# Second feed-forward in passes of 6, 13 and 13 token tiles, with two sequences split between passes

## The chip, the cores and the metric

The kernel runs on one core of a Trainium2 chip. The metric is the device time of one execution in microseconds (us). Three runs of the kernel before gave 700.61, 701.8 and 703.71 us; their median, 701.8 us, is the time before.

## The reference

Eight sequences of 512 tokens with 128 features go through a feed-forward with experts, an attention, and the same feed-forward again, each added to its input:

```python
x = x + 0.5 * ffn(layernorm(x))        # router, 8 experts of 128 -> 512 -> 128, each token to its best two
x = x + attention(layernorm(x))        # 16 heads of 8, causal
x = x + 0.5 * ffn(layernorm(x))        # the same weights

# ffn(x):
logits = x @ router_w + router_b
topk_scores, topk_idx = top_k(logits, 2)
gates = softmax(topk_scores)
# for each expert e of a token's two:  y += gate_e * (relu(x @ W1[e] + b1[e]) @ W2[e] + b2[e])
```

All arrays are float32.

## The kernel before, in words

The kernel computes each expert only for the tokens that chose it. A sequence is four tiles of 128 tokens (`T` = 4). A *pass* (class `Group`, L449) takes some sequences, gives each expert a room of `cap` rows in a buffer in DRAM (`xs`), scatters every normalised token to two of these rooms, and runs the eight experts over their rooms. There are six passes (L1362 to L1367): f0, f1, f2 for the first feed-forward, g0, g1, g2 for the second. The f and the g passes each take two, three and three whole sequences, with rooms of 351, 480 and 480 rows. A room is computed in `ct` tiles of equal size: 351 is three tiles of 117 rows, 480 is four of 120.

`route` (L801) does one sequence of a pass: layernorm, transposes, router logits, rank of each expert, and a running count that gives each token its row in its two rooms (`to`, L866); `seen` carries the counts from one sequence of the pass to the next. It then enters eight scatters (`scatter`, L874), one for each tile and rank, as jobs for GpSimd (POOL). `close_group` (L916) checks that no room overflowed. If one did, a flag set in `verdict` (L1272) sends the program to the general path (L1549), which computes everything densely.

`experts` (L924) is a generator of *pieces*. For an expert e, `turn` (L972) transposes the room's tiles on TensorE (lines L976 and L980, tiles xbT_ps and xT), four pieces `wide` (L986, tile z, L989) multiply by a quarter of W1 and evict with ReLU on ScalarE (L996) or VectorE (L998), and `ct` pieces `out` (L1010, tile y, L1013) multiply by W2 and add the bias on VectorE (L1017, tile ysb). The pieces of expert e + 1's first part and expert e's `out` pieces alternate. `pieces` (L461) is their number: 65 for g0, 73 for each pass of 480 rows. The rows come from DRAM by `fetch` (L931, tile xb), issued on SP.

The results go back in two ways. An untagged pass (f0, f1, f2, g0) stores each expert's room in order (L1024, SP), and `combine` (L1064) gathers two rows for each token with indirect DMAs on GpSimd (`gather`, L1084) and adds them to x with the gates (`add`, L1071). A tagged pass (g1, g2) carries with each row its destination; `homes` (L939) computes it, `send` (L956) scatters the results token by token with indirect DMAs on GpSimd, and `collect` (L1099) loads them for a whole sequence from SP (tile yr, L1110), adds on VectorE (L1114) and stores the output (L1120).

The order is written out by hand in `macaron_kernel`. Attention is 96 units (8 sequences x 4 groups of heads x 3 steps, L1394); before it lie 30 units without attention, after it 30 more (`first`, `core`, `tail`, `ends`, L1399). `plan` (L1421) says which pass lends its pieces to which units:

```python
        plan = [
            (f0, first, first, -16), (f1, -17, -16, 7), (f2, 5, 7, 43), (g0, 41, 43, 79),
            (g1, 78, 79, tail - 1), (g2, tail - 2, tail - 1, ends),
        ]
```

The second number is the unit in which rooms are fetched first, the third and fourth bound the units that take pieces. `surround` (L1427) builds a unit: the scores on TensorE (`scores`, L1192, lines L1201 and L1208), the values of the unit before (L1227), one piece, the causal mask, then what is due in this unit (parts of `route`, `project`, `operands`, `finish`, put there by `at`), and further pieces up to the quota, which is the pieces left over the units left, rounded up. So g0's 65 pieces fill 36 units. One scatter, gather or send is issued in each unit by `transfer` (L650), more if they are urgent. Each waits for the latest eviction in the program's order (`mark`, `behind_mark`, L635). VectorE, ScalarE, TensorE and SP follow the order of the program.

Other names that the steps touch: rooms are listed in `ROOMS` (L49) with the number of sequences, the rows and whether tagged; g0 reuses f1's. `clear` (L687) and `clear_results` (L705) zero the rooms of g1 and g2 and their results early in the attention (`later`, L557).

Of the kernel before, what the change touches and what calls it, by code (L numbers as in the profile page):

```python
# [13 lines left out]
I32 = mybir.dt.int32  # L14
# [34 lines left out]
ROOMS = [(2, 351, False), (3, 480, False), (3, 480, False), (3, 480, True), (3, 480, True)]  # L49
# [399 lines left out]
class Group:  # L449


    def __init__(self, seqs, cap, key, xs, ys, tagged):
        self.seqs, self.cap, self.key, self.xs, self.ys = seqs, cap, key, xs, ys
        self.tagged, self.width = tagged, D + 2 * tagged
        self.ct = -(-cap // P)
        self.rows = cap // self.ct
        assert self.ct * self.rows == cap
        self.parts = [(t, min(3 if cap > 4 * P else 4, self.ct - t))
                      for t in range(0, self.ct, 3 if cap > 4 * P else 4)]
        self.placed = 0  # L460
        self.pieces = E * (len(self.parts) * (1 + C) + self.ct) + 1  # L461
# [21 lines left out]
class Main:  # L483
    def __init__(self, tc, ctx, aps):
# [37 lines left out]
        for i, (n, cap, tagged) in enumerate(ROOMS):  # L522
            self.xs.append(self.tc.dram_tile([E * n * N, D + 2 * tagged], FP, name=f"xs_{i}"))

            self.ys.append(self.tc.dram_tile(
                [2 * n * N * tagged + E * cap, D], FP, name=f"ys_{i}"
            ))
# [80 lines left out]
        self.ops, self.o_tok, self.normal, self.whole = {}, {}, {}, {}  # L608
# [96 lines left out]
    def clear_results(self, i):  # L705
        dst = self.ys[i][: 2 * ROOMS[i][0] * N, :].rearrange("(p a r) d -> p a (r d)", p=P, r=4)
        self.nc.sync.dma_start(
            dst, self.zeros[:, : 4 * D].unsqueeze(1).to_broadcast([P, dst.shape[1], 4 * D])
        )
# [80 lines left out]
    def open_group(self, seqs, cap, i, key):  # L790
        const = self.const
        g = Group(seqs, cap, key, self.xs[i], self.ys[i], ROOMS[i][2])
        assert len(seqs) <= ROOMS[i][0] and cap <= ROOMS[i][1]
        assert not g.tagged or cap == ROOMS[i][1]
        g.to = const.tile([P, len(g.seqs), T, 2], I32, name=f"to_{key}")
        g.back = const.tile([P, len(g.seqs), T, 2], I32, name=f"back_{key}")
        g.gates = const.tile([P, len(g.seqs), T, 2], FP, name=f"gates_{key}")
        g.seen = const.tile([P, E], BF, name=f"seen_{key}")
        return g

    def route(self, g, i, urgent=False, ahead=False, early=False):  # L801

        nc, small, tc = self.nc, self.small, self.tc
        b = g.seqs[i]
        key = f"{g.key}_{b}"
        if b in self.normal:
            xn = self.normal.pop(b)
        else:
            xn = yield from self.layernorm(self.x[b], key)
# [34 lines left out]
        nc.tensor.matmul(pos, self.earlier, mask, start=True, stop=False)  # L844
        for t in range(T - 1):
            nc.tensor.matmul(
                pos[:, t + 1 :, :], self.ones,
                mask[:, t : t + 1, :].to_broadcast([P, T - 1 - t, E]),
                start=False, stop=(i == 0 and t == T - 2),
            )  # L850
        if i > 0:
            nc.tensor.matmul(
                pos, self.ones, g.seen.unsqueeze(1).to_broadcast([P, T, E]),
                start=False, stop=True,
            )
# [10 lines left out]
        nc.vector.tensor_reduce(g.to[:, i], sm, AX.X, ALU.max)  # L866
        nc.vector.tensor_scalar(g.back[:, i], g.to[:, i], E * g.cap - 1, None, ALU.min)
        if g.tagged:
            nc.vector.tensor_copy(xn[:, :, D], g.to[:, i, :, 0])
            nc.vector.tensor_scalar(  # L870
                xn[:, :, D + 1], self.place, float(2 * N * i), None, ALU.add
            )

        def scatter(t, r):  # L874
            ins = nc.gpsimd.indirect_dma_start(  # L875
                out=g.xs[:, :],
                out_offset=bass.IndirectOffsetOnAxis(ap=g.to[:, i, t, r : r + 1], axis=0),
                in_=xn[:, t, : g.width], in_offset=None,
            ).ins
            tc.declare_no_dep(ins, group=f"xs_{g.key}", reason="no row has two tokens")  # L880
            tc.add_to_no_dep_group(f"xs_{g.key}", ins)
            self.in_turn(ins, scatter=True)
            self.behind_mark(ins)
            g.placed += 1

        self.enter([partial(scatter, t, r) for t in range(T) for r in range(2)], urgent, ahead)

        with nc.allow_low_precision(reason="counts of at most 32, exact in bf16"):
            by_e = mask.rearrange("p t e -> p e t")
            if i == 0:  # L890
                nc.vector.tensor_reduce(g.seen, by_e, AX.X, ALU.add)
            else:
                more = small.tile([P, E], BF, tag="more", name=f"more_{key}")
                nc.vector.tensor_reduce(more, by_e, AX.X, ALU.add)
                nc.vector.tensor_tensor(g.seen, g.seen, more, ALU.add)
# [16 lines left out]
        nc.vector.reciprocal(g.gates[:, i, :, 0], tot)  # L912
        nc.vector.tensor_tensor(g.gates[:, i, :, 1], g.gates[:, i, :, 0], e2, ALU.mult)
        yield

    def close_group(self, g, k):  # L916

        assert g.placed == 2 * T * len(g.seqs)
        nc = self.nc
        cp = self.bank([P, 512], f"cnt_ps_{g.key}")  # L920
        nc.tensor.matmul(cp[:1, :E], self.ones[:, 0:1], g.seen, start=True, stop=True)
        nc.vector.tensor_scalar(self.counts[:, k], cp[:1, :E], -float(g.cap), None, ALU.add)

    def experts(self, g):  # L924
# [14 lines left out]
        def homes(e, xb):  # L939
# [12 lines left out]
                home[e][:rows, : g.ct], row, float(2 * N * len(g.seqs) + e),  # L952
# [111 lines left out]
    def combine(self, g, i, dst=None, urgent=False, ahead=False):  # L1064

        nc = self.nc
        b = g.seqs[i]
        x = self.x[b]
        self.whole[b] = False

        def add(t, yts):  # L1071
            for r in range(2):
                nc.vector.scalar_tensor_tensor(
                    x[:, t, :], yts[r], g.gates[:, i, t, r : r + 1], x[:, t, :],
                    ALU.mult, ALU.add,
                )
            if t == T - 1:
                self.whole[b] = True
                if dst is not None:
                    nc.sync.dma_start(dst[b].rearrange("(t p) d -> p t d", p=P), x)  # L1080
# [3 lines left out]
        def gather(t, r):  # L1084
# [4 lines left out]
                    ap=g.back[:, i, t, r : r + 1], axis=0  # L1089
# [6 lines left out]
        self.enter([partial(gather, t, r) for t in range(T) for r in range(2)], urgent, ahead)  # L1096
        yield

    def collect(self, g, i, dst, parts=1):  # L1099

        nc = self.nc
        b = g.seqs[i]
        x = self.x[b]
        if i % 2 == 0:
            self.pair = self.p2.tile([P, 2, T, 2, D], FP, tag="ee", name=f"yr_{b}")
        yr = self.pair[:, i % 2]
        src = g.ys[2 * N * i : 2 * N * (i + 1), :].rearrange("(t p r) d -> p t r d", p=P, r=2)
        n = T // parts
        for k in range(parts):
            nc.sync.dma_start(yr[:, ts(k, n)], src[:, ts(k, n)])  # L1110
        yield
        for t in range(T):
            for r in range(2):
                nc.vector.scalar_tensor_tensor(  # L1114
                    x[:, t, :], yr[:, t, r], g.gates[:, i, t, r : r + 1], x[:, t, :],
                    ALU.mult, ALU.add,
                )
            if t % n == n - 1:
                k = t // n
                nc.sync.dma_start(  # L1120
                    dst[b].rearrange("(t p) d -> p t d", p=P)[:, ts(k, n)], x[:, ts(k, n)]
# [5 lines left out]
    def project(self, b):  # L1127
# [4 lines left out]
        assert self.whole[b], b  # L1132
# [171 lines left out]
def macaron_kernel(  # L1304
# [51 lines left out]
    with ExitStack() as main:  # L1356
# [5 lines left out]
        f0 = m.open_group([0, 1], 351, 0, "f0")  # L1362
        f1 = m.open_group([2, 3, 4], 480, 1, "f1")
        f2 = m.open_group([5, 6, 7], 480, 2, "f2")
        g0 = m.open_group([0, 1], 351, 1, "g0")
        g1 = m.open_group([2, 3, 4], 480, 3, "g1")
        g2 = m.open_group([5, 6, 7], 480, 4, "g2")  # L1367
        order = [f0, f1, f2, g0, g1, g2]
        place = {True: {}, False: {}}
        for g in order:  # L1370
            for i, b in enumerate(g.seqs):
                place[g.key[0] == "f"][b] = (g, i)
# [32 lines left out]
        def routed(u, g, i, urgent=False, ahead=False):  # L1405
            early = u < 0 or u > core
            r = m.route(g, i, urgent, ahead, early)
# [4 lines left out]
            if g is not f1:  # L1412
# [68 lines left out]
        with m.banks(("m", 8)):  # L1481

            n = [m.normalise(b) for b in range(5)]
            r = [m.route(f0, 0, early=True), m.route(f0, 1, early=True), m.route(f1, 0, True, early=True)]
# [11 lines left out]
            routed(first + 1, f1, 1, urgent=True)  # L1496
            routed(first + 3, f1, 2, urgent=True)
            routed(-22, f2, 0, urgent=True)
            combined(-16, f0, 0, urgent=True, ahead=True)
            routed(-14, f2, 1, urgent=True)  # L1500
            combined(-12, f0, 1, urgent=True)
            routed(-10, f2, 2, urgent=True)
            at(-10, m.project(0), 8)
            for b in range(B):
# [3 lines left out]
                elif b > 2:  # L1508
                    combined(u - (17 if b == 5 else 21), *place[True][b], urgent=b == 5, ahead=b == 5)
# [5 lines left out]
                routed(u + seq + (3 if b == B - 1 else 4), *place[False][b], urgent=b in (1, 4, 5, 6, 7), ahead=b in (4, 6, 7))  # L1515
            for i in range(2):
                combined(79 + 7 * i, g0, i, out)
            for i in range(3):
                at(tail + 2 + 3 * i, m.collect(g1, i, out), 5)
# [13 lines left out]
        with m.banks(("m", 8)):  # L1533
# [7 lines left out]
            last = [m.collect(g2, i, out, parts=2) for i in range(3)]  # L1541
# [55 lines left out]
```

## Time and profile before

| what | value |
|---|---|
| median of three runs | 701.8 us |
| profiled execution, its own time | 700.09 us |
| its span, first to last instruction | 698.3 us |
| mean granted TensorE clock | 0.977 |
| TensorE matmul busy | 629.2 us, 90% |
| f2 pass, first transpose to g0's first | 178.56 to 341.54 us |
| g0 pass, first transpose to g1's first | 341.54 to 493.97 us |
| g1 pass, its first transpose to its last matmul | 493.97 to 612.0 us |
| g2 pass, its first transpose to its last matmul | 616.69 to 677.5 us |
| last scatter of results lands | 683.35 us |

A page of the profile has the busy time of each engine, then the span in 40 slices (a digit is the busy share in tenths), the DMA queues, the chain of work that ended last, and the costliest groups of instructions. In the timeline each row is: start, duration, engine, line, operation, output<-inputs, shape, count, and in brackets the idle time before it with what ended it. Matmuls are pipelined, so durations of TensorE rows overlap; the start of the next row tells what one costs. A float32 matmul is recorded as two instructions, so a z piece has x2 and a y tile, four matmuls, has x8.

### The profile page before, as it was taken

How to read it: one execution, taken by the hardware profiler on the slowest of the kernel's cores; microseconds unless marked ns; L12 is line 12 of the kernel's file. 1: busy time of each engine (PE TensorE's matmuls, PEld its weight loads, DVE VectorE, ACT ScalarE, POOL GpSimd, SP SyncE). 2: the span in 40 equal slices, each digit the busy share in tenths (PEclk: the TensorE clock that was granted, in tenths of full speed). 3: DMA queues.
4: the chain of work that ended last, by engine and by line, in shares of the span. 5: the costliest groups of instructions: out<-in, count | busy, mean ns of one | idle time of the engine just before them, and what ended most of it. 6: DMA issues, size and time to landing. Idle time of an engine off the chain costs nothing. (4 is left out here: it accounts for less than half of the span.)

```text
span 698.3 us, 13045 instructions
## 1 busy us (share of the span) xinstructions
PE 629.2 (90%) x4867; PEld 410.3 (59%) x4867; DVE 410.2 (59%) x1442; ACT 341.3 (49%) x548; POOL 300.3 (43%) x322
## 2 busy tenths in 40 slices
PE   3269999999999999999999999999999998969980
PEld 2148867756465656556656656656456656747760
DVE  6736448734466666675687677676666654433414
ACT  4034443455755656565665565555665552234420
POOL 3744637642223223314154423424144556575660
PEclk9999999999999999999999999999999999889995
DMA  8747843312409921111211111101402111145324
GB/s 265 197 136 209 205 115 98 85 45 77 101 22 172 264 69 38 30 29 43 71 32 49 40 38 38 30 27 39 105 27 75 35 31 42 53 121 140 104 58 143
DMA packets 78670, 61.06 MB, mean 87 GB/s; under 512 B 7392, under 2 KB 70792, under 8 KB 78600
## 3 DMA queue, kind: packets, MB, share of 16 engines
q1 hardware_dynamic: 69608, 42.51, 23.8%
q0 software_dynamic: 8704, 17.63, 8.5%
q8 instruction: 41, 0.67, 0.4%
q14 instruction: 29, 0.24, 0.1%
q10 hardware_dynamic: 288, 0.01, 0.0%
HBM read 26.34 MB, written 33.78 MB: 86 GB/s over the span
## 5 line engine op out<-in xcount | busy, mean ns | idle before, releaser
L1208 ACT ACTIVATE ee<-st 128x768 f32<-128x768 f32 (+1 forms) x192 | 159.0, 881 | 104.1 <-PE st L1201 100.6
L474 POOL DMA_INDIRECT yt_f<-ys,back_f x64 | 64.8, 1013 | 133.5 <-DVE ee L1215 55.7
L1215 DVE TENSOR_TENSOR ee<-ee,keep 128x256 f32<-128x256 f32 (+1 forms) x192 | 93.5, 507 | 25.4 <-ACT ee L1208 25.3
L1013 PEld LDWEIGHTS y_g<-w_sb,h_g 128*120 128x120 f32 (+1 forms) x704 | 87.1, 184 | 27.4 <-issue 21.7
L875 POOL DMA_INDIRECT xs<-xn_g,to_g x64 | 63.8, 998 | 90.1 <-DVE ee L1215 34.9
L1013 PEld LDWEIGHTS y_f<-w_sb,h_f 128*120 128x120 f32 (+1 forms) x704 | 85.9, 182 | 28.5 <-issue 16.2
L1201 PE MATMUL st<-qT,kT 32*128 32x512 f32 (+3 forms) x1024 | 96.1, 467 | 2.3 <-ACT h_f L996 0.8
L1013 PE MATMUL y_f<-w_sb,h_f 128*120 128x128 f32 (+1 forms) x704 | 93.9, 277 | 0.2 <-DVE h_f L998 0.2
L989 PE MATMUL z_g<-xT_g,w_sb 128*128 128x480 f32 (+1 forms) x192 | 92.6, 569 | 1.3 <-ACT xT_g L980 1.3
L1013 PE MATMUL y_g<-w_sb,h_g 128*120 128x128 f32 (+1 forms) x704 | 93.0, 277 | 0.6 <-DVE o_tok L1250 0.3
L1227 PE MATMUL o<-ee,vpad 128*32 128x512 f32 (+3 forms) x1024 | 89.4, 442 | 0.8 <-DVE ee L1215 0.8
L989 PE MATMUL z_f<-xT_f,w_sb 128*128 128x480 f32 (+1 forms) x192 | 88.8, 551 | 1.0 <-ACT xT_f L980 1.0
L996 ACT ACTIVATE h_f<-z_f,b1T 128x480 f32<-128x480 f32 (+1 forms) x86 | 53.5, 623 | 68.2 <-PE z_f L989 67.3
L957 POOL DMA_INDIRECT ys<-ysb_g,home_g x64 | 63.7, 996 | 39.3 <-ACT h_g L996 8.7
L1017 DVE TENSOR_TENSOR ysb_f<-y_f,b_sb 120x128 f32<-120x128 f32 (+1 forms) x88 | 25.0, 287 | 77.9 <-PE y_f L1013 74.2
L996 ACT ACTIVATE h_g<-z_g,b1T 128x480 f32<-128x480 f32 (+1 forms) x71 | 45.7, 646 | 47.4 <-PE z_g L989 46.7
L1201 PEld LDWEIGHTS st<-qT,kT 32*128 32x128 f32 x1024 | 43.1, 183 | 32.6 <-issue 8.1
L1017 DVE TENSOR_TENSOR ysb_g<-y_g,b_sb 120x128 f32<-120x128 f32 (+1 forms) x88 | 25.1, 287 | 58.2 <-PE y_g L1013 57.6
L1227 PEld LDWEIGHTS o<-ee,vpad 128*32 128x32 f32 x1024 | 23.5, 108 | 52.4 <-issue 7.5
L875 POOL DMA_INDIRECT xs<-xn_n,to_f x40 | 39.0, 974 | 34.9 <-ACT xi_sb L727 8.1
L989 PEld LDWEIGHTS z_g<-xT_g,w_sb 128*128 128x128 f32 x192 | 30.1, 195 | 26.6 <-issue 15.2
L989 PEld LDWEIGHTS z_f<-xT_f,w_sb 128*128 128x128 f32 x192 | 30.2, 194 | 13.8 <-issue 7.2
(186 smaller groups left out, 778.7 us busy)
## 6 DMA issues: line engine op xcount, KB each, us to landing
w_sb<-in_L_ffn_W_dram SPq DMA_DIRECT2D x16, 256.0 KB
xs<-zeros SPq DMA_DIRECT2D x8, 487.5 KB
xb_g<-xs SPq DMA_DIRECT2D x16, 243.8 KB
xb_f<-xs SPq DMA_DIRECT2D x16, 240.0 KB
ys<-ysb_f SPq DMA_DIRECT2D x16, 240.0 KB
ys<-zeros SPq DMA_DIRECT2D x2, 1536.0 KB
x<-in_L_attn_x_dram SPq DMA_DIRECT2D x8, 256.0 KB
xs<-zeros SPq DMA_DIRECT2D x1, 1920.0 KB
```

What stands on the lines that cost most here:

```text
L474: ins = op(*args, **kw)
L875: ins = nc.gpsimd.indirect_dma_start(out=g.xs[:, :], out_offset=bass.IndirectOffsetOnAxis(ap=g.to[:, i, t, r : r + 1], axis=0), in_=xn[:, ...
L957: ins = nc.gpsimd.indirect_dma_start(out=g.ys[:, :], out_offset=bass.IndirectOffsetOnAxis(ap=home[e][:rows, t : t + 1], axis=0), in_=ys[:r ...
L989: nc.tensor.matmul(z[:, :n], self.w1_sb[:, e, ts(c, P)], xT[:, n0 : n0 + n], start=True, stop=True,)
L996: ins = nc.scalar.activation(dst, z[:, :n], AF.Relu, bias=bias)
L1013: nc.tensor.matmul(y[:rows], h[:, c, ts(t, rows)], self.w2_sb[:, e, c, :], start=(c == 0), stop=(c == C - 1),)
L1017: ins = nc.vector.tensor_tensor(ys[:rows, t, :], y[:rows], self.b2_sb[:rows, e], ALU.add)
L1201: nc.tensor.matmul(st[:, h, c0 : c0 + N - kt * P], kT[r0 : r0 + SLOT, ts(kt, P)], qT[r0 : r0 + SLOT, kt * P :], start=True, stop=True,)
L1208: nc.scalar.activation(ee[:, two, :width], st[:, two, :width], AF.Exp)
L1215: ins = self.nc.vector.tensor_tensor(d, d, self.keep.unsqueeze(1).unsqueeze(1).to_broadcast([P, 2, len(parts), P]), ALU.min,)
L1227: self.nc.tensor.matmul(self.o[h * SLOT : (h + 1) * SLOT, kt * P :], self.vpads[b % 2][:, kt, 4 * g + h, :], ee[:, h, c0 : c0 + n], start= ...
```

## The change

The second feed-forward's passes are cut by tiles instead of by sequences. Of the 32 tiles g0 takes 6 (sequence 0 and half of sequence 1), g1 takes 13 (the other half of sequence 1, sequences 2 and 3, three tiles of sequence 4), g2 takes 13 (the last tile of sequence 4, sequences 5, 6, 7). The rooms of g0 are 256 rows, those of g1 and g2 512, so an expert is computed in 2, 4 and 4 full tiles of 128 rows, ten in all. The passes of the first feed-forward stay as they are.

A pass now holds `shares`, each a sequence with its first and last tile. The rank sums in `route` restart at each share; a split sequence's scatters go to two rooms. The lists `to`, `back` and `gates` belong to the sequence instead of the pass. `combine` and `collect` work on a share's tiles: the second half of sequence 1 comes through g1's tagged results instead of gathers, and g1 and g2 each have four collects instead of three. Clearing covers 13 tiles and 512 rows; results are cleared in rows of 256 elements instead of 512.

```diff
-ROOMS = [(2, 351, False), (3, 480, False), (3, 480, False), (3, 480, True), (3, 480, True)]
+ROOMS = [(8, 351, False), (12, 480, False), (12, 480, False), (13, 512, True), (13, 512, True)]
...
     def clear_results(self, i):
-        dst = self.ys[i][: 2 * ROOMS[i][0] * N, :].rearrange("(p a r) d -> p a (r d)", p=P, r=4)
+        dst = self.ys[i][: 2 * ROOMS[i][0] * P, :].rearrange("(p a r) d -> p a (r d)", p=P, r=2)
...
-        nc.tensor.matmul(pos, self.earlier, mask, start=True, stop=False)
-        for t in range(T - 1):
...
+        for g, i in shares:
+            _, t0, t1 = g.shares[i]
+            sums = [(pos[:, t0:t1], self.earlier, mask[:, t0:t1])]
+            for t in range(t0, t1 - 1):
+                sums.append((
+                    pos[:, t + 1 : t1, :], self.ones,
+                    mask[:, t : t + 1, :].to_broadcast([P, t1 - 1 - t, E]),
+                ))
+            if i > 0:
+                sums.append((
+                    pos[:, t0:t1], self.ones,
+                    g.seen.unsqueeze(1).to_broadcast([P, t1 - t0, E]),
+                ))
...
-        self.enter([partial(scatter, t, r) for t in range(T) for r in range(2)], urgent, ahead)
+        self.enter([
+            partial(scatter, g, t, r) for g, i in shares
+            for t in range(*g.shares[i][1:]) for r in range(2)
+        ], urgent, ahead)
...
     def combine(self, g, i, dst=None, urgent=False, ahead=False):
...
-        self.enter([partial(gather, t, r) for t in range(T) for r in range(2)], urgent, ahead)
+        self.enter(
+            [partial(gather, t, r) for t in range(first, end) for r in range(2)], urgent, ahead
+        )
...
     def collect(self, g, i, dst, parts=1):
...
-        src = g.ys[2 * N * i : 2 * N * (i + 1), :].rearrange("(t p r) d -> p t r d", p=P, r=2)
-        n = T // parts
-        for k in range(parts):
-            nc.sync.dma_start(yr[:, ts(k, n)], src[:, ts(k, n)])
+        src = g.ys[: 2 * P * g.tiles, :].rearrange("(t p r) d -> p t r d", p=P, r=2)
+        n = -(-(end - first) // parts)
+        for t in range(first, end, n):
+            rows = slice(t - first + g.base[i], t - first + g.base[i] + n)
+            nc.sync.dma_start(yr[:, t : t + n], src[:, rows])
...
-        g0 = m.open_group([0, 1], 351, 1, "g0")
-        g1 = m.open_group([2, 3, 4], 480, 3, "g1")
-        g2 = m.open_group([5, 6, 7], 480, 4, "g2")
+        g0 = m.open_group([(0, 0, T), (1, 0, 2)], 256, 1, "g0")
+        g1 = m.open_group([(1, 2, T), *whole(2, 3), (4, 0, 3)], 512, 3, "g1")
+        g2 = m.open_group([(4, 3, T), *whole(5, 6, 7)], 512, 4, "g2")
...
-            for i in range(3):
-                at(tail + 2 + 3 * i, m.collect(g1, i, out), 5)
+            for i, (_, t0, t1) in enumerate(g1.shares):
+                at(tail + 2 + 3 * i, m.collect(g1, i, out), 1 + t1 - t0)
...
-            last = [m.collect(g2, i, out, parts=2) for i in range(3)]
+            last = [m.collect(g2, i, out, parts=min(2, g2.shares[i][2] - g2.shares[i][1])) for i in range(4)]
```

## The prediction, as made before the result

> **What bounds the kernel now.** I read the page first (span, busy shares, PEclk), then the timeline of TensorE for the boundaries of the passes, then busy time by stage between those boundaries, and last the chain that ended last. From the page:
>
> ```profile
> span 698.3 us, 13045 instructions
> PE 629.2 (90%) x4867; PEld 410.3 (59%) x4867; DVE 410.2 (59%) x1442; ACT 341.3 (49%) x548; POOL 300.3 (43%) x322
> PE   3269999999999999999999999999999998969980
> PEclk9999999999999999999999999999999999889995
> ```
>
> TensorE is full from the fifth slice to the 34th and no other engine is near that. The stages, cut at the first transposes of a pass (178.56, 341.54, 493.97), at the end of attention (575.95), at the first transpose of g2 (616.69) and at the end of the last scatter (681.55):
>
> ```profile
> 178.56:341.54 162.98, 162.48 (x1375) 95.50 (x1371) 102.70 (x321) 98.06 (x155) 47.18 (x46) 1.00 0.36 86
> 341.54:493.97 152.43, 149.87 (x1319) 90.50 (x1316) 110.03 (x352) 88.46 (x145) 54.88 (x54) 1.00 0.15 43
> 493.97:575.95 81.98, 79.96 (x669) 47.57 (x666) 51.57 (x167) 46.52 (x71) 36.75 (x36) 1.00 0.17 46
> 575.95:616.69 40.74, 32.68 (x197) 25.43 (x195) 16.05 (x72) 9.65 (x17) 26.41 (x28) 0.90 0.21 59
> 616.69:681.55 64.86, 60.14 (x354) 44.69 (x354) 22.93 (x88) 25.64 (x40) 43.11 (x44) 0.95 0.39 103
> ```
>
> Columns: window, its length, then busy PE, PEld, DVE, ACT, POOL, the clock, DMA. The first two rows are the f2 pass and the g0 pass, each beside 36 attention units: TensorE is busy 162.5 of 163.0 and 149.9 of 152.4 us, so the length of these stages is TensorE's work. In 575.95:616.69 it is not (32.7 of 40.7): there the last sequence is routed and scattered, and g2 waits for that. g2 itself is TensorE's again. Then come sends, loads, additions:
>
> ```profile
> 680.57 2.78 DMA ys<-ysb_g,home_g
> 683.37 2.52 DMA yr<-ys
> ```
>
> **What the Trainium skill says.** "TensorE: Matmul & The Clock Gate", section "Back-to-back issue gap", prices a stream by the moving columns, N/2.4 + 2.5 ns, not by the stationary rows. The first half holds here in kind: a y tile of 117 or 120 rows takes the same 277 ns a record. The size does not: 480 columns would be 202 ns, and the two records of an f32 z of 480 take 0.81 us start to start, 405 each. I use the trace. The same page, section "What's actually happening", halves the clock after an idle window of about 3.4 us. The trace has it at half speed in 591.2 to 598.0 and 615.1 to 621.9, after idle stretches of TensorE of 1.9 and 4.7 us; no gap of 0.7 us in attention did that. "PSUM — Partial Sum Buffer", section "Engine vs sequencer instructions", calls the VectorE and GpSimd queues strict FIFO; the trace agrees, GpSimd idled 4.0 us for a VectorE that stood 5.6 us before an addition. "DMA: Bandwidth & Descriptors", section "Anatomy of one DMA", fits 2.0 us + bytes/436e3: 2.6 us for the 256 KB load that took 2.52.
>
> **The change part by part.** *g0 pass.* Prices are start to start, since the busy times overlap:
>
> ```profile
> 455.87 0.86 PE L989 MATMUL z_g<-xT_g,w_sb 128*128 128x351 f32 x2
> 456.56 1.04 PE L1013 MATMUL y_g<-w_sb,h_g 128*117 128x128 f32 x8
> 457.53 0.93 PE L1201 MATMUL st<-qT,kT 32*128 32x384 f32 x8
> ...
> 539.57 0.97 PE L989 MATMUL z_g<-xT_g,w_sb 128*128 128x480 f32 x2
> 540.47 0.94 PE L1201 MATMUL st<-qT,kT 32*128 32x256 f32 x16
> ```
>
> A z of 351 columns costs 0.69, a y tile 0.97, a z of 480 costs 0.90. Summed so over the whole stage, the 24 y tiles of g0 take 23.9 us (0.995 each), its 32 z 23.0 (0.72), its 8 turns 3.5 (0.43); in f2 the 32 y, 32 z and 8 turns take 31.5, 29.0 (0.905) and 3.9. A z of 256 by that slope (0.186 us for 129 columns) is 0.58, by the columns' full pace (1.7 ns for both records) 0.56; I take 0.57. The change removes 8 y tiles (8 x 0.995 = 8.0), narrows 32 z by 0.15 (4.8) and 8 turns by 95 columns at 0.85 ns (0.6): -13.4 us.
>
> *What covers less.* g0 has 65 pieces, 8 x (5 + 3) + 1, in 36 units: two a unit to unit 71, one in the last 7. It will have 57: two to unit 63, one in 15 units. A unit with one piece has nothing behind its last step, and TensorE then waits:
>
> ```profile
> 469.39 0.93 PE L1201 MATMUL st<-qT,kT 32*128 32x384 f32 x8 [0.48 <-ACT ee L1208]
> 477.28 1.14 PE L1201 MATMUL st<-qT,kT 32*128 32x512 f32 x8 [0.72 <-ACT kT L1184]
> ```
>
> The size comes from f2 against g0: the pieces differ by 64.4 - 50.4 = 14.0 us, g0's stage has one more routing on TensorE (+1.3), so g0 should be 12.7 shorter and is 10.5: 2.1 us lost in 7 units, 0.3 each. Eight more such units: +2.4. Ends: 0 if other steps cover, 8 x 0.7 = 5.6 if each unit has the whole gap. The stage: -11.0.
>
> *g1 and g2 passes.* 512 columns instead of 480: a z +0.054 (32 columns at 1.7 ns), a turn +0.03; y unchanged, 128 moving columns as before, ScalarE's eviction of 0.66 grows likewise but has a second idle to each. In attention g1 has 17 z and 5 turns: +1.0. After attention g2's start hangs on the chain finish, layernorm, logits, 8 scatters, fetch; 7 z stand in TensorE's queue ahead of its steps, one at half clock, and the scatters wait for evictions: +0.4. TensorE's own end of g1 (612.0) has 4.7 us of slack, so the other z are free; without that slack they cost 0.4. The fetch, 128 rows for 120: +0.2 of 3.3. g2: 32 z (1.7), 8 turns (0.2), 4 z at half clock twice (0.2): +2.2.
>
> *End.* 26 additions for 24 at 0.33: +0.65. The first load is one tile, 128 KB, 2.3 us by the page's fit instead of 2.52: -0.2. One DMA more among loads and among stores on SP lies beside additions. The last four sends wait for the same evictions in both programs. +0.4.
>
> *Moved, at no cost.* Four gathers of g0 and their additions become rows of g1's load: 4 x 1.3 us of GpSimd's turns, so g1's sends end some 5 us sooner against g2 and VectorE's 5.6 us stand before the first addition shrinks. TensorE never waited for it (busy 55.1 of 55.1 us in 621.9 to 677), so no gain. SP gets a new wait: the store of sequence 1's second half now stands before the second and third load and the fetches of experts 6 and 7. It waits for an addition near 637; expert 6's transposes came at 654.5, so 15 us of cover; past it, g2 would wait us for us. VectorE waits for those loads too, covered as the 5.6 us were. The clears of rooms grow by 8 x 32.5 and 2 x 128 KB and the latter go in rows of 1 KB instead of 2: SP's, near 200 to 250, under TensorE work; 0, at most 3 us (516 KB at the 166 GB/s there). Splitting the rank sums adds a few bf16 matmuls of 0.1 us and takes as many away.
>
> Sum: -11.0 + 1.0 + 0.4 + 0.2 + 2.2 + 0.4 = -6.8. The profiled execution took 700.1 us (span 698.3, 1.8 around it); on it 693.3. The median shown is 1.7 higher: 701.8 - 6.8 = **695.0**.
>
> **The rivals.** *Full pace*: one-piece units are covered by routing, projection and the like, the gap costs nothing: -13.4 + 4.2 = -9.2, 692.6. For: the st records cost the same in both stages. Against: kT and qT took 1.85 us more in g0 than in f2. *Half*: each new one-piece unit has the whole gap of 0.7 (5.6 us) and VectorE, idle 0.03 us in the unit with the rotation, holds two units by some 0.5: -13.4 + 6.6 + 4.2 = -2.6, 699.2. *Slower*: attention units have a floor. Scores, exponential, next scores share one PSUM buffer; were the floor the present mean of 152.4/36 = 4.23 us, the shorter pieces would only make TensorE wait, and the +4.2 of the longer passes would stand: 706.0. It decides once the wait eats 9.2 us of the 13.4, 0.26 us a unit over all 36. Against: units of one piece ran in 3.0 to 4.25 us. *It doesn't do what it says*: an expert with more rows than its room sends the program down the general path, at many times the time. From the reference and its inputs the fullest expert gets 207, 459 and 470 rows; excluded.
>
> **How the numbers follow.** Forecast (692.7 to 697.5) 0.60; full pace or more 0.15; half 0.18; slower 0.07. The range takes in full pace with a us of its own, 691.3, and half, 699.5. A measurement can tell about 0.5% (3.5 us) from no change: faster below 698.3 (forecast, full pace, half of half), slower above 705.3.
>
> **What would show it.** The g0 stage, first transposes to first transposes, at 141.4 us instead of 152.4, with y_g x16 tiles there; idle of TensorE before st and qkv of 4 to 5 us in it; 494 to the end of attention at 83; g2's first transpose to its last matmul 63 instead of 60.8; the chain's last piece 26 additions. Wrong would be a g0 stage above 144, a wait of xbT for the fetch inside g2, or TensorE waiting on VectorE near the loads.

## The result, and the profile after

Four runs of the changed kernel gave 695.02 to 695.26 us, median **695.16 us**, against 701.2 us of the kernel before (the three runs named above and one of 700.49): a ratio of 0.9907, 95% interval 0.9881 to 0.9933. The forecast was 695.0. The profiled execution took 695.02 us with a span of 693.2 us, at a mean granted clock of 0.98. From its page:

```profile
span 693.2 us, 12906 instructions
PE 622.7 (90%) x4797; PEld 402.8 (58%) x4797; DVE 406.3 (59%) x1432; ACT 343.3 (50%) x552; POOL 295.7 (43%) x318
...
PE   3269999999999999999999999989999998989970
...
PEclk9999999999999999999999999999999999989995
```

TensorE is 6.5 us less busy (622.7 for 629.2) and as full as before in its share; VectorE has ten instructions fewer. The same stages as before, cut at the first transposes of f2, of g0, of g1, at the end of attention, at the first transpose of g2, at the end of the last scatter's issue (columns: window, length, busy PE, PEld, DVE, ACT, POOL, the clock, DMA share, GB/s):

```profile
180.18:343.15 162.97, 162.47 (x1374) 95.49 (x1370) 102.97 (x324) 98.05 (x155) 47.16 (x46) 1.00 0.39 89
343.15:486.19 143.04, 137.61 (x1248) 81.65 (x1244) 104.59 (x341) 88.33 (x149) 55.36 (x54) 1.00 0.15 43
486.19:570.25 84.06, 82.04 (x673) 48.44 (x670) 51.32 (x165) 47.13 (x71) 36.56 (x37) 1.00 0.16 46
570.25:608.61 38.36, 31.92 (x194) 24.20 (x192) 15.59 (x69) 10.02 (x16) 25.83 (x27) 0.95 0.18 54
608.61:676.20 67.59, 62.97 (x354) 45.66 (x354) 24.09 (x90) 26.69 (x40) 38.86 (x40) 0.95 0.35 104
```

The f2 stage, which the change leaves alone, took 162.97 us for 162.98. The g0 stage is the gain. Its busy time fell by 12.3 us and its length by only 9.4: TensorE now stands 5.4 us in it, where it stood 2.6. For the other stages the end of attention has to be cut at the same instruction in both traces; in the one before that is 576.28, a third of a us later than the prediction had it. Then:

| stage (us) | before | after | difference | predicted |
|---|---|---|---|---|
| start, up to f2's first transpose | 178.56 | 180.18 | +1.6 | 0 |
| f2 pass | 162.98 | 162.97 | 0 | 0 |
| g0 pass | 152.43 | 143.04 | -9.4 | -11.0 |
| g1 in attention | 82.31 | 84.06 | +1.75 | +1.0 |
| end of attention to g2's first transpose | 40.41 | 38.36 | -2.05 | +0.6 |
| g2, first transpose to last matmul | 60.79 | 63.64 | +2.85 | +2.2 |
| end | 20.84 | 20.99 | +0.1 | +0.4 |
| span | 698.3 | 693.2 | -5.1 | -6.8 |

The gain of the medians is 6.0 us, that of these two executions 5.1. The chain that ended last still goes last send, load, additions (start, duration, what):

```profile
675.16 2.48 DMA ys<-ysb_g,home_g
677.66 0.34 SPq L1140
678.06 2.77 DMA yr<-ys
```

It follows the second load, two tiles. The first, one tile, was asked for earlier and landed first.

*Where TensorE stands in the g0 stage.* Its waits of 0.15 us or more there (line waiting, what it waited for, us in total, times, longest):

```profile
PE st L1231 <- ACT kT L1214: 3.3, 8, 0.7
PE st L1231 <- ACT ee L1238: 1.5, 3, 0.6
PE qkv_ps_a L1169 <- DVE o_tok L1280: 0.4, 2, 0.2
```

Before there were five such waits, 1.9 us in all: 0.7 once for kT, 0.5 once for ee, 0.7 in three for o_tok. Now there are thirteen, in two kinds of units. Five are long, 0.64 to 0.73 us, and all of these lie in units with one piece. Two such units on TensorE's timeline:

```profile
446.97 0.64 PE L1208 MATMUL kT_ps<-ident,kpad 128*128 128x128 f32 x4
448.29 1.14 PE L1231 MATMUL st<-qT,kT 32*128 32x512 f32 x8 [0.67 <-ACT kT L1214]
449.36 0.86 PE L1257 MATMUL o<-ee,vpad 128*32 128x256 f32 x16
450.14 0.70 PE L1013 MATMUL z_g<-xT_g,w_sb 128*128 128x256 f32 x2
451.48 0.93 PE L1231 MATMUL st<-qT,kT 32*128 32x384 f32 x8 [0.64 <-ACT ee L1238]
```

The transposes of the keys (kT_ps) are the last thing TensorE has before the next unit's scores (st). ScalarE must first bring them out of PSUM (kT, L1214), and nothing lies in between: 0.67 us. In the next unit the one piece, a z, is issued right behind the values (o), its time is over before the exponential (ee) is through, and the scores wait again, 0.64 us.

The other eight are short, 0.18 to 0.29 us, and seven of them lie in units that still have two pieces. What stands behind the keys' transposes there is mostly one z, and this is narrower now. The same place before and then after:

```profile
349.19 0.76 PE L989 MATMUL z_g<-xT_g,w_sb 128*128 128x351 f32 x2
350.02 1.14 PE L1201 MATMUL st<-qT,kT 32*128 32x512 f32 x8
```

```profile
350.37 0.60 PE L1013 MATMUL z_g<-xT_g,w_sb 128*128 128x256 f32 x2
351.21 1.14 PE L1231 MATMUL st<-qT,kT 32*128 32x512 f32 x8 [0.24 <-ACT kT L1214]
```

The z of 351 columns left a gap of 0.08 us (brackets begin at 0.15), that of 256 leaves 0.24. With the gaps under 0.15 us counted, the units with one piece (the last 7 of the 36 before, the last 15 after) went from 1.34 to 3.68 us of idle TensorE, those with two from 1.22 to 1.75.

*Start and clock.* The start is the same program in both kernels, yet 1.6 us longer. The four z from 44 us on (eight records), before and then after:

```profile
43.98 3.09 PE L989 MATMUL z_f<-xT_f,w_sb 128*128 128x351 f32 x8
```

```profile
43.99 4.63 PE L1013 MATMUL z_f<-xT_f,w_sb 128*128 128x351 f32 x8
```

The rows around them say why: in both traces the z ahead of these, at 42.07, takes 1.54 us, and later ones, from 48.22 and 49.77 on, take 0.76, so TensorE begins at half its pace. The trace's record of the granted clock begins where the full pace does, at 45.1 us before and at 48.2 after (a view prints 1.00 for the time ahead of the first entry); 3.1 us more at half pace cost 1.55. Later, while there is work for TensorE, the clock is halved twice in each of these two executions. Before it was 6.8 us from 591.2 (after a gap of TensorE of 1.87 us, where the last sequence is routed) and 6.8 us from 615.1 (after a gap of 4.7, where g2 waits for its rows). After:

```profile
587.50:590.90 3.40, 3.40 (x16) 2.53 (x15) 2.65 (x11) 1.20 (x2) 2.19 (x2) 0.50 0.14 43
608.00:614.80 6.80, 5.52 (x13) 2.98 (x13) 4.12 (x11) 1.86 (x3) 5.24 (x6) 0.50 0.72 210
```

The first of the two is half as long, which is worth 1.7 us of the 2.05 that the stretch after attention became shorter. The rest is g2's fetch: from its issue to g2's first transpose it was 3.37 us before (from 613.32) and 2.97 after (from 605.64).

### The profile page after: what moved, and what is told of

Its sections match the earlier page's. It is cut to its first block, busy times and chain, and to the rows that moved or that the text cites. A ratio compares the mean times of both kernels' runs of the same rounds, so it can differ in the third digit from the quotient of the medians.

```text
span 693.2 us, 12906 instructions
## 1 busy us (share of the span) xinstructions
PE 622.7 (90%) x4797; PEld 402.8 (58%) x4797; DVE 406.3 (59%) x1432; ACT 343.3 (50%) x552; POOL 295.7 (43%) x318
## 5 line engine op out<-in xcount | busy, mean ns | idle before, releaser
L1037 PEld LDWEIGHTS y_g<-w_sb,h_g 128*128 128x128 f32 x640 | 81.6, 193 | 32.1 <-issue 25.3
L1013 PE MATMUL z_g<-xT_g,w_sb 128*128 128x512 f32 (+1 forms) x192 | 90.1, 556 | 1.4 <-DVE e_g L933 0.7
L1013 PE MATMUL z_f<-xT_f,w_sb 128*128 128x480 f32 (+1 forms) x192 | 90.4, 560 | 1.0 <-ACT xT_f L1004 1.0
L1037 PE MATMUL y_g<-w_sb,h_g 128*128 128x128 f32 x640 | 86.3, 280 | 0.5 <-DVE o_tok L1280 0.3
L1020 ACT ACTIVATE h_g<-z_g,b1T 128x512 f32<-128x512 f32 (+1 forms) x77 | 49.4, 643 | 54.7 <-PE z_g L1013 54.5
L1041 DVE TENSOR_TENSOR ysb_g<-y_g,b_sb 128x128 f32<-128x128 f32 x80 | 23.1, 290 | 78.0 <-PE y_g L1037 69.4
```

The source lines that it names most:

```text
L1013: nc.tensor.matmul(z[:, :n], self.w1_sb[:, e, ts(c, P)], xT[:, n0 : n0 + n], start=True, stop=True,)
L1020: ins = nc.scalar.activation(dst, z[:, :n], AF.Relu, bias=bias)
L1037: nc.tensor.matmul(y[:rows], h[:, c, ts(t, rows)], self.w2_sb[:, e, c, :], start=(c == 0), stop=(c == C - 1),)
L1041: ins = nc.vector.tensor_tensor(ys[:rows, t, :], y[:rows], self.b2_sb[:rows, e], ALU.add)
```

## The experiments

The theory on record: the shorter pieces of g0 give about what they were costed at, less what TensorE loses in units with one piece; the wider passes cost what their columns cost; the split does nothing by itself. The rivals: the split of the sequences gives something itself (fewer gathers, other loads), or attention units have a floor that the pieces can't go under. The first four kernels ran beside 27 runs of the kernel before (median 702.56 us), the other four beside seven (701.58 us). Medians of different sessions differ by about a us, so ratios to the kernel before are compared. In the durations of stages read from the traces that plays no part.

**e1: the split and the wider g1 and g2, but rooms of 351 rows in g0.**

```diff
-        g0 = m.open_group([(0, 0, T), (1, 0, 2)], 256, 1, "g0")
+        g0 = m.open_group([(0, 0, T), (1, 0, 2)], 351, 1, "g0")
```

> The changed kernel with g0's rooms at 351 rows (three tiles of 117) again; the split of 6, 13 and 13 tiles and the rooms of 512 stay. Theory (the gain is g0's narrower pieces on TensorE): the g0 stage goes back from 143.0 to about 152.4 us, TensorE's idle in it from 5.4 to about 2.6, and the time to 695.2 + 9.4 = 704.6, above the kernel before, since the wider g1 and g2 stay. Rival (the split itself gains, by fewer gathers and an earlier end of the sends): the time stays within 2 us of 695.2.

Measured: 707.46 us (704.85 to 709.0, eight runs), ratio 1.0064 (1.0043 to 1.0084). The g0 stage took 152.47 us with TensorE busy 149.92, as before the change, and its waits were those of before (kT 0.7, ee 0.5, o_tok 0.7). g1 in attention took 84.06 and g2 63.57, as in the changed kernel. So the whole gain of the g0 stage is in its tiles, and without it the program is slower than before, by what the other passes lost. That the median lies some 3 us above the expected one, the stages don't explain; in this execution the half-clock window after attention was 6.8 us (596.9 to 603.7), not 3.4, and the start 1.6 us longer, with a window of half clock of its own (the clock is the third number from the end):

```profile
95.10:98.50 3.40, 3.40 (x9) 1.99 (x8) 0.00 (x0) 1.88 (x3) 0.00 (x0) 0.50 0.61 127
```

The eight runs go with the clock: the two with a mean granted clock of 0.980 and 0.981 took 704.85 and 705.22 us, near what was expected, the six with 0.975 to 0.978 took 706.6 to 709.0. The kernel before was also 1.4 us slower beside these runs (702.56) than beside those of the changed kernel (701.2).

**e2: the split and 256 rows in g0, but 480 in g1 and g2.**

```diff
-ROOMS = [(8, 351, False), (12, 480, False), (12, 480, False), (13, 512, True), (13, 512, True)]
+ROOMS = [(8, 351, False), (12, 480, False), (12, 480, False), (13, 480, True), (13, 480, True)]
...
-        g1 = m.open_group([(1, 2, T), *whole(2, 3), (4, 0, 3)], 512, 3, "g1")
-        g2 = m.open_group([(4, 3, T), *whole(5, 6, 7)], 512, 4, "g2")
+        g1 = m.open_group([(1, 2, T), *whole(2, 3), (4, 0, 3)], 480, 3, "g1")
+        g2 = m.open_group([(4, 3, T), *whole(5, 6, 7)], 480, 4, "g2")
```

> The changed kernel with rooms of 480 rows (four tiles of 120) for g1 and g2; g0 keeps 256. Theory (32 more columns in each z cost TensorE 0.054 us each, in attention and in g2): the g1 part of attention 1.5 us shorter, g2's first transpose to its last matmul about 2 us shorter, the time 695.2 - 3.8 = 691.4. Rival (the wider pieces fall into time in which TensorE waits anyway): the time stays within 1 us of 695.2.

Measured: 693.63 us (690.53 to 694.39, four runs), ratio 0.9875 (0.9845 to 0.9905). The g0 stage, g1 in attention and g2:

```profile
342.43:485.48 143.05, 137.62 (x1249) 81.65 (x1245) 104.59 (x341) 88.33 (x149) 55.33 (x54) 1.00 0.15 41
485.48:567.80 82.32, 80.32 (x673) 47.92 (x670) 51.06 (x165) 46.62 (x71) 36.88 (x36) 1.00 0.18 47
...
607.26:667.90 60.64, 59.98 (x354) 44.58 (x354) 23.69 (x89) 25.64 (x40) 35.81 (x37) 0.96 0.41 106
```

The stages did what was expected: g0 as in the changed kernel, g1 1.7 and g2 3.0 us shorter. The whole time did not. By ratio it is 0.3% below the changed kernel, where 4.7 us would be 0.7%, and the two intervals overlap. Of the difference 1.1 us is in the stretch after attention (39.46 for 38.36), where this execution again had the window of 6.8 us. The full rows of g1 and g2 are a cost, then, whose size in the whole time this run alone leaves open; e6 below comes back to it.

**e3: the split alone**, with rooms of 351, 480 and 480 rows (both edits above).

> Only the split of 6, 13 and 13 tiles, with the old rooms: 351 rows for g0, 480 for g1 and g2. Theory (the split alone leaves TensorE's pieces as they were, and what it saves on GpSimd and VectorE is off the path): 700.5 to 702, no change from before; g0 stage 152.4. Rival (the split has a gain or a cost of its own, four collects, one more wait in SP's queue, fewer gathers): 2 us or more away from the kernel before, on either side.

Measured: 702.05 us (700.05 to 705.07, twenty runs), ratio 0.999 (0.9977 to 1.0003). Its g0 stage:

```profile
343.07:495.53 152.46, 149.91 (x1321) 90.59 (x1317) 110.17 (x353) 88.42 (x145) 54.89 (x54) 1.00 0.16 44
```

This is the stage of the kernel before to 0.03 us, and g1 (82.32) and g2 (61.41) are within 0.7 of it. Four gathers fewer, a collect more, other clears and split rank sums come to nothing that twenty runs can tell: the interval leaves room for 1.6 us of gain and 0.2 of cost. So the rival that the split has a gain or a cost of 2 us or more falls.

**e4: in a unit with one piece, that piece goes after the unit's other steps**, not before them. It was made to measure the lost cover by giving some of it back.

```diff
+            late = att and quota == 1
+            mode = m.evac
-            run(take(fill, 1 if quota else 0))
+            run(take(fill, 1 if quota and not late else 0))
             m.evac = "act"
...
-            todo = max(quota - 1, 0)
+            todo = 1 if late else max(quota - 1, 0)
...
+            if late:
+                m.evac = mode
             run(take(fill, todo))
+            m.evac = "act"
```

> The changed kernel; in attention units that have one piece only, the piece comes after the unit's other steps instead of ahead of them. Theory (in such units TensorE waits for the copy of kT and for the exponential because nothing stands behind the last step): these waits, 4.8 us in the g0 stage, fall below 2 us, the g0 stage goes to 140 to 141, the time to 692.5 to 693.5. Rival (a unit has a floor of its own, the wait only moves, to the values or the transposes that now stand closer behind the scores): g0 stage 143, time within 0.7 of 695.2.

Measured: 692.77 us (692.72 to 693.41, four runs), ratio 0.9862 (0.9834 to 0.9891). The g0 stage and TensorE's waits in it:

```profile
343.73:483.46 139.73, 136.29 (x1248) 81.01 (x1244) 105.63 (x341) 87.89 (x149) 56.22 (x54) 1.00 0.14 41
```

```profile
PE st L1231 <- ACT kT L1214: 1.6, 6, 0.4
PE st L1231 <- ACT ee L1238: 1.5, 3, 0.6
```

The stage is 3.3 us shorter with the same instructions on TensorE, a little more than was expected, although the waits did not fall below 2 us. The edit acts on units with one piece only. Of the three waits for kT there, 0.67, 0.68 and 0.73 us, two are gone, where a y tile now stands between the transposes and the scores, and one fell to 0.42, where a z does. The first of them:

```profile
445.68 0.63 PE L1208 MATMUL kT_ps<-ident,kpad 128*128 128x128 f32 x4
446.15 1.06 PE L1037 MATMUL y_g<-w_sb,h_g 128*128 128x128 f32 x8
447.13 1.14 PE L1231 MATMUL st<-qT,kT 32*128 32x512 f32 x8
```

The five other waits for kT, 0.19 to 0.29 us, lie in units with two pieces and are as before the edit. Those for ee stayed.

**e5: the keys and queries of a group of heads one unit earlier**, where the group is not a sequence's first. The pieces stay where they were.

```diff
-                at(u + g * per - 2, m.operands(b, g), 2)
+                at(u + g * per - (3 if g else 2), m.operands(b, g), 2)
```

> The changed kernel; the transposes and copies of queries and keys for the next group of heads come one attention unit earlier (not for the first group of a sequence), pieces stay where they are. Theory (the largest part of TensorE's idle in the g0 stage is the wait of the scores for the copy of kT, 3.3 us in 8 places): this wait falls below 1 us, the g0 stage goes from 143.0 to about 140.5, the time to about 692.7. Rival (the unit has a floor of its own and the wait goes over to the exponential or to VectorE): kT's wait falls and others rise by as much, stage 142.5 to 143.5, time within 0.7 of 695.2.

Measured: 693.28 us (692.58 to 694.9, four runs), ratio 0.9873 (0.984 to 0.9906); the g0 stage took 140.32 us. Its waits:

```profile
PE st L1231 <- ACT kT L1214: 1.1, 3, 0.7
PE st L1231 <- ACT ee L1238: 1.1, 3, 0.6
PE o L1257 <- DVE ee L1245: 0.7, 1, 0.7
```

Another remedy for the same wait, and the same stage shortened by 2.7 us. The wait is 1.1 us, just above the 1 that was expected. Five of the eight waits for kT are gone, and one for the masked exponential is new. Two different edits, one that puts a piece behind the keys' transposes and one that moves these ahead, give back 3.3 and 2.7 us. So this lost cover is most of what the stage fell short of its pieces' saving. Not all of it had been counted as waiting: idle time fell by 2.0 us in both, busy time by 1.3 and 0.7.

**e6: e4 and the 480 rows of e2.**

> The late piece of the one-piece units and rooms of 480 rows for g1 and g2 together, on the changed kernel. If the two terms lie in different stages they add: g0 stage 139.7, g1 part of attention 82.3, g2 near 60.7, time 692.8 - 3.8 = 689.0. If they share their gain (TensorE's shorter pieces in g1 only lengthen its wait for the last routing): 691 or more.

Measured: 689.01 us (687.57 to 689.1, four runs), ratio 0.9806 (0.9777 to 0.9836). The g0 stage 139.87, g1 in attention 82.33, g2 60.72 us: the two edits add up. Against e4 the ratio is 0.56% lower, 3.9 us; the two intervals just touch. The stages of the two traces give 1.7 and 2.65 us, less 0.9 by which the stretch after attention is longer here. Three pairs differ in the rooms of g1 and g2 alone: by their ratios the full rows cost 5.2 us (e1 and e3, whose intervals are well apart), 3.9 (e4 and e6) and 2.2 (the changed kernel and e2). That they cost something is shown; their price in the whole time is 2 to 5 us, and the expected 3.8 lies in the middle.

**e7: e6 and the early keys of e5.**

> Late piece, 480 rows and early keys together. With the keys early and the piece late, nothing but the exponential should hold TensorE in one-piece units: g0 stage about 138.5, time about 688. If VectorE, which is full in the units with the rotation, is the floor: no better than late piece and 480 rows alone.

Measured: 686.99 us (685.9 to 688.2, four runs), ratio 0.9772 (0.9739 to 0.9805). The g0 stage:

```profile
344.61:482.89 138.28, 135.95 (x1248) 81.14 (x1244) 105.60 (x341) 88.65 (x149) 56.61 (x54) 1.00 0.14 40
```

TensorE idles 2.3 us in it, less than the 2.6 of the kernel before, and is busy 13.9 us less than there. The stage is 14.1 us shorter than before the change: the gross saving of the prediction, 13.4 us, is there once the pieces are covered. In the whole time the intervals of e6 and e7 overlap.

**e8: e6 with dummy matmuls on TensorE**, six in the gap where the last sequence is routed and fifteen in the one before g2's first rows. Nobody reads their result; they only keep TensorE running.

```diff
+    def warm(self, n, name):
+        wp = self.bank([P, 512], f"warm_{name}")
+        for _ in range(n):
+            self.nc.tensor.matmul(
+                wp.rearrange("p (a b) -> p a b", b=P), self.ones,
+                self.ones.unsqueeze(1).to_broadcast([P, 4, P]), start=True, stop=True,
+            )
...
+            self.warm(6, "route")
...
+                        m.warm(15, "fetch")
```

> Late piece and 480 rows, and in addition matmuls of constants that nobody reads: 6 of 512 bf16 columns where TensorE waits for the last sequence's layernorm, 15 where it waits for g2's first fetch. Theory (the g2 stage, the stretch after attention and the start vary by 1.7 or 3.4 us because idle TensorE loses half its clock for one or two windows of 3.4 us): no half clock near 582 to 612, g2's first transpose to its last matmul 57.5 to 58 instead of 60.7, the stretch from attention's end to g2 1 to 2 us shorter, time 684 to 686. Rival (the half clock hurts nobody, as TensorE catches up while others wait): within 1 us of the same kernel without these matmuls.

Measured: 685.72 us (683.56 to 687.53, four runs), ratio 0.9754 (0.9716 to 0.9793). The stretch after attention and g2:

```profile
565.16:605.19 40.03, 37.04 (x214) 27.02 (x212) 15.29 (x69) 9.64 (x16) 26.09 (x27) 0.91 0.18 53
605.19:663.76 58.57, 57.92 (x354) 43.48 (x354) 23.92 (x89) 25.49 (x40) 36.05 (x37) 1.00 0.43 110
```

Half of it worked in the execution that was traced. g2 ran at a clock of 1.00 throughout and is 2.15 us shorter than in e6 (60.72), though not the 57.5 to 58 that was expected. The stretch before it was expected 1 to 2 us shorter and was not (39.56 in e6): although the six matmuls cut the gap ahead of the transposes from 1.85 to 0.65 us, the clock was halved for 6.8 us from 580.6 all the same. The traced run, of 686.38 us, had a mean granted clock of 0.981, as one of 687.53 had 0.979; the other two, of 683.56 and 685.07, had 0.988, so in these the first window may have been spared too, which no trace shows. The medians of e7 and e8 lie below both kernels, e8's the lowest; in the whole time the intervals of e8 overlap with those of e6 and e7, so that the half clock costs time is shown by g2's stage, not by the medians.

## Why the prediction was right

The number came out within 0.2 us. The steps behind it did so less exactly, and that they sum to it so closely is luck: errors cancel.

*The g0 pass: right in kind, short in its second term.* The pieces did what was said. Summed start to start over the stage, waits apart, the y tiles fell from 23.9 to 16.0 us (7.9; predicted 8.0), the z from 22.4 to 17.8 (4.7; predicted 4.8) and the turns from 3.3 to 2.5 (0.9; predicted 0.6): 13.4 us in all, the predicted sum. Busy time fell by 12.3 all the same, because rows that the change doesn't touch took 1.1 us more: the transposes of the layernormed rows (xnT_ps_a) 0.4, the projections (qkv_ps_a) 0.3, the values (o) and the queries' transposes (qT_ps) 0.2 each. Why they did isn't shown; in e7 busy time is 13.9 us below the kernel before. Idle time grew by 2.9 us where 2.4 was predicted. Of this 2.3 lies where the prediction put it, in eight more units with one piece, 0.3 each as predicted. The other 0.5 lies in the units with two pieces, where the narrower z covers less; there the prediction had nothing. So two terms are missing from the stage, 1.1 us busy and 0.5 us idle, and they make up the 1.6 between 11.0 and 9.4.

The stage ended at 143.0, not 141.4, still inside the bound of 144 that was set for it, and TensorE stood 4.8 us before st and 0.4 before qkv where 4 to 5 in all was said. *Full pace* falls by the waits. *Half* falls by their number: only five waits in the fifteen units with one piece are as long as the whole gap, and the fifteen together stand 3.7 us. The *floor* falls by the stage, which became 9.4 us shorter at the same number of units, and by e7, where it is 4.8 us shorter still.

*The wider passes: +4.6, where +3.2 was predicted, of it some 0.5 by the clock.* A z of 512 costs what was said, 0.86 us start to start where one of 480 takes 0.81, 1.7 ns a column: the 20 z of g1 in attention went from 18.0 to 19.1 us. But there are 20 and six turns, as both traces count, and not 17 and five. The other steps of g1's +1.75 are 0.2 for the turns, 0.2 for transposes in the attention's own rows, and 0.3 for the 16 y tiles, which went from 15.6 to 15.9 us. "y unchanged" was the step that failed here: a y tile of 128 rows costs 0.02 us more than one of 120. In e2, with 120 rows, the y tiles take 15.6 again. In g2 a z and a y follow each other every 1.75 us (1.68 with 480 rows in e2), so 32 pairs give +2.2, the turns +0.25, and the rest of the +2.85 is that the half clock after the fetch reaches about a us further into g2 than before. In pairs of kernels that differ in the rooms alone the full rows cost g2 3.0 (after and e2), 2.65 (e4 and e6) and 2.2 us (e1 and e3).

*The stretch after attention: the sign was wrong.* +0.6 was predicted and -2.05 came. The wider z are there, but the first window of half clock was 3.4 us in place of 6.8, which is worth 1.7. The fetch, predicted 0.2 longer for its 128 rows, took 0.4 us less from issue to first transpose, for which no reason is shown. The prediction held both windows as given.

*The end: +0.1 for +0.4.* The first load, of 128 KB, landed 2.05 us after its issue, 0.5 sooner than the 256 KB before, not 0.2. The page "DMA: Bandwidth & Descriptors" of the Trainium skill, section "Anatomy of one DMA — SWDGE (gpsimd) path", fits 2.0 us and a part that grows with the bytes to DMAs that GpSimd issues, which as an estimate would be 2.3 us for 128 KB; these loads are issued on SP, and the trace decides. VectorE then stood once more, between the first load and the second:

```profile
679.71 0.74 DVE L1144 SCALAR_TENSOR_TENSOR x<-yr,gates_g,x 128x128 f32<-128x128 f32 x2 [7.13 <-DMA yr<-ys]
680.86 7.89 DVE L1144 SCALAR_TENSOR_TENSOR x<-yr,gates_g,x 128x128 f32<-128x128 f32 x24 [0.41 <-DMA yr<-ys]
```

So the 26 additions took 9.03 us from first to last, 1.14 more than the 24 of before, not 0.65. What paid for it: from the last send's issue to the first addition it was 4.55 us, not 5.34 (0.3 by the send, 2.48 for 2.78, and 0.5 by the load), and 0.2 less from the last matmul to that send.

*Moved, at no cost: right.* e3 shows it in the whole time. The new wait on SP is there: the store of sequence 1's second half was issued at 629.40, the load behind it at 629.82, the fetches of experts 6 and 7 at 630.39. Expert 6's transposes began at 655.82, 25 us later, and in g2 TensorE waited for a fetch only at the first one.

*What cancelled.* In the profiled execution g0 gave 1.6 us too little, the passes of 512 rows cost 1.4 too much and the start, which no part of the change touches, 1.6; against that stand 2.65 in the stretch after attention and 0.3 at the end. The sum is -5.1, 1.7 short of -6.8. This execution is 5.1 us below the 700.09 that the sum was made against; the rest of the agreement is that the median before, 701.8, was 1.7 above that execution, while the runs after lay within 0.24 us of each other. Against the median of all four runs before, 701.2, the gain is 6.0 us, not 6.8.

*What stays open.* The clock. The page "TensorE: Matmul & The Clock Gate" of the Trainium skill, section "What's actually happening", says that the window of about 3.4 us in which activity is watched runs freely and doesn't start with the kernel. The traces agree: in all ten, every change of the clock lies a whole number of 3.413 us after the first entry of the record (in the changed kernel 158, 159, 164, 166 and 184 of them), and that first entry lies anywhere from 45.1 to 48.6 us. The same gap is therefore cut differently by the windows of each execution. A place that all ten kernels share shows what this does, where TensorE waits for f1's first rows, near 92 us. In e1, e5 and e7 one window there has 1.61, 1.69 and 1.81 us of busy TensorE, and the clock is halved in the next one; in the other seven it has 1.84 us or more, and the clock stays.

The page also says that the clock falls after an idle window; here a window that was about half idle was enough. At the routing gap after attention, six traces have 1.2 to 1.6 us of busy time in the window, and the clock is halved for 6.8 us from its end; the changed kernel, e4 and e5 have 1.8, and it is halved for 3.4 us, one window later. e8, with 1.9 us, was halved for 6.8 us and doesn't fit; what decides in it wasn't found. A window of half clock is worth 1.7 us. In e1 the runs' own clocks go with their times, so this is likely most of the 3 us by which it missed its expected median. In e2 they don't: 690.53 and 694.35 us both came at 0.977, and its miss of 2 us stays open.

## What to carry to other kernels

Where one engine's work is spread as filler over steps that wait for other engines, shorter filler saves its gross time only as long as something still lies between each step and its dependent one. Count the units that will have too little, price them from a stage that has some already, and look for a place further back in the unit for what little there is: here that alone gave back 3.3 us of the 4.0 by which the stage fell short. Shorter pieces also cover less where their number stays the same. Ask which pieces cost by the tile and which by the column: here a y tile took 1.0 us with 117 rows and with 128, so g0 gained by having 16 of them in place of 24, and a z costs by its columns, so it gained by rooms of 256, and the padding of the other two passes to 512 rows took some 4 of the 9.4 us back, which rooms of 480 rows avoid.

## What was not expected of the hardware

- Once the clock was up, windows of 3.41 us in which TensorE was busy for 1.8 us or less were followed by half clock, for 3.4 or for 6.8 us, in all ten traces; in e7 gaps of 1.04 and 0.56 us close together were enough. Half clock costs up to half its length. Fifteen matmuls in a gap of 4 us in front of g2 prevented it and shortened g2 by 2.15 us; six in the gap of 1.85 us did not in the one execution that was traced.
- Ten executions of the same first stretch reached f2's first transpose at 178.56 to 182.01 us, most of it through the phase of that clock. It sets how well a change of a us or two can be told from one profile.
- A TensorE row in front of a wait of 0.6 to 0.7 us shows 0.16 to 0.2 us more than the same row in a stream (a z of 256 columns 0.70 for 0.54, the transposes of a kT up to 0.64 for 0.44), and this shows as busy time, not as waiting.
